# A transformer block on one core: sources turned by 64-row products, maxima by products with the identity in column groups

## The chip, the cores and the metric

The kernel runs on one core of a Trainium2 chip. The metric is the device time of one execution in microseconds. TensorE (PE in the profile; its weight loads are PEld) does the matrix products, VectorE (DVE), ScalarE (ACT) and GpSimd (POOL) the rest, and SyncE (SP) issues nearly all transfers.

## The reference

Sixteen batches of 256 tokens of width 256 pass through one block: self-attention with 16 heads of 16, cross-attention to a context of 256 tokens, and an MLP of width 1024. Layer norms are modulated by a projection of the condition.

```python
def _ln(x):
    mu = jnp.mean(x, axis=-1, keepdims=True)
    var = jnp.var(x, axis=-1, keepdims=True)
    return (x - mu) * jax.lax.rsqrt(var + LN_EPS)
...
c_proj = jax.nn.silu(c) @ W_mod + b_mod
shift_a, scale_a, gate_a, shift_m, scale_m, gate_m = jnp.split(c_proj, 6, axis=-1)
x_norm = modulate(_ln(x), shift_a, scale_a)
qkv = x_norm @ W_qkv + b_qkv
...
attn_w = jax.nn.softmax(jnp.einsum('bhqd,bhkd->bhqk', q, k) * scale, axis=-1)
attn_out = jnp.einsum('bhqk,bhkd->bhqd', attn_w, v)
...
x = x + gate_a[:, None] * attn_out
q_c = _ln(x) @ W_qc + b_qc
kv_c = _ln(context) @ W_kvc + b_kvc
...
x = x + c_attn_out
x_norm2 = modulate(_ln(x), shift_m, scale_m)
h = jax.nn.gelu(x_norm2 @ W_mlp1 + b_mlp1)
x = x + gate_m[:, None] * (h @ W_mlp2 + b_mlp2)
```

## The kernel before

A unit is one attention of one batch: kind "s" for self, "c" for cross. There are 32 units in the list `seq` (line 791): five "s", then "s" and "c" in turn, and five "c" at the end. The MLP of all batches comes after them, with some of its loads and first products among the last units.

The main loop (line 1268) goes over the units n and, within each, over eight beats k (`beat`, line 1103). `keep_in_program_order` holds each engine to the order in which the code issues. A beat handles several units at once:

- **S** (`s_tile`, line 697): scores of unit n + 1 with queries on the partitions, four products of 63 rows, two in each half of the array's rows, into the two banks of the tile `s`. One instruction of DVE then takes the row maxima out of both banks into `u.mx` (tile mx). The next S writes the same two banks.
- **T** (`t_part`, line 741): the transposed scores of unit n, four products of 64 rows into the two banks of the tile `st`. The 64th row carries the negative maximum, so that the exponential on ScalarE (`exp`, line 752) needs no other shift. The next T writes the same banks. The function `visit` (line 1079) issues S, then what it is given as `between`, then T.
- **o** (`av_part`, line 771): in beats 0, 2, 4 and 6, sixteen value products of 128 rows in four column groups of 32.
- **The lanes** (`lane`, `lanes`, `run`, lines 451 to 480): in beats 1, 3, 5 and 7, the projections to q, k, v and the output projection of neighbouring units. Each is cut into two halves of 64 rows; the first half of one operation (upper rows of the array) and the second half of another (lower rows) are issued in turn, twelve products of each, 24 in all.
- **The turning of a source** (`transposed`, line 377): the normalized input of a unit, 256 tokens by 256 features, is transposed by four 128-row products with the identity into one bank (tile psT). Each unit turns one source for unit n + 3 (`q3.T[0]`), half of it in beat 0 and half in beat 2, once the source is marked ready; a unit whose n + 3 is a "c" (`lx`) turns a second one, `lx.T[1]`, whole, in beat 4. ScalarE reads the result in beat 3, or 6.
- **The maxima** (`m_turn`, `m_row`, `m_part`, lines 725 to 739): in beat 0 and beat 4 a half of the maxima, 128 x 16, is transposed by one product (into the second half of the source's bank, a bank psm of its own, or `st`). ScalarE negates it into `m`, and one transfer by SP writes it to the 64th rows of the queries, where T reads it four beats later.

In beat 0 the order on TensorE is S, T, o, maxima, half a turning; in beat 2 S, T, o, half a turning; in beat 4 S, T, o, second source, maxima; in beat 6 S, T, o and one pair of lane products. Ahead of S in beats 0 and 4 ScalarE is given the upper parts of K and Q (`high`, tiles h_k, h_q and the like), so they stand in its queue ahead of the beat's exponential.

Of the kernel before, what the change touches and what calls it, by code (L numbers as in the profile page):

```python
# [10 lines left out]
F32 = mybir.dt.float32  # L11
# [5 lines left out]
P = 128  # L17
# [4 lines left out]
def pixart_block(  # L22
# [53 lines left out]
    DVE.memset(wz, 0.0)  # L76
    ident = const.tile([P, P], F32, name="ident")
    make_identity(nc, ident)
    mhalf = const.tile([P, 2], F32, name="mhalf")
# [297 lines left out]
    def transposed(src, name, scale=None, pool=False):  # L377

        o = Box()

        def place():
            o.ps = ps_gen(f"psT_{name}", SHORT)

        def turn(fs=range(KC)):
            if len(fs) == KC:
                place()
            for f in fs:
                for t in range(NT):
                    PE.transpose(o.ps[:, f * N + t * P:f * N + (t + 1) * P],
                                 src()[:, t, f * P:(f + 1) * P], ident)  # L390

        def high():
            hi = work.tile([P, KC, N], F32R, tag="xTh", name=f"xTh_{name}", bufs=4)
            lo = work.tile([P, KC, N], F32R, tag="xTl", name=f"xTl_{name}", bufs=4)
            o.xT = (hi, lo)
            if scale is None:
                ACT.copy(hi.rearrange("p k n -> p (k n)"), o.ps)
            else:
                for f in range(KC):
                    ACT.activation(hi[:, f], o.ps[:, f * N:(f + 1) * N], AF.Identity, scale=scale[f])  # L400

        def low():
            hi, lo = o.xT
            if scale is None:
# [66 lines left out]
    def lanes(x, y):  # L471


        if x:
            x.ps, x.fresh = ps_gen(f"ps_{x.name}", LONG if x.tok else SHORT), True
        return zip_longest(*(lane(o, half) for half, o in enumerate((x, y)) if o))

    def run(steps, n=12):
        for _ in islice(steps, n):
# [2 lines left out]
    def to_stack(W, src, bias, dst, which, name):  # L482
# [24 lines left out]
        def low():  # L507
            if name == "k0":
                gap(work, 64, "gap_l")
            o.lo = work.tile([P, KC, N], F32R, tag="qkl", name=f"l_{name}", bufs=3)  # L510
            if name == "k0":
                gap(work, 192, "gap_mx")
# [184 lines left out]
    def s_tile(u, g, par, t, bank=None, home=sp):  # L697
# [30 lines left out]
    def m_turn(u, hf, pst=None):  # L728

        if pst is None:  # L730
            pst = ps_gen(f"psm_{u.n}_{hf}", SHORT)
        PE.transpose(pst[:16, :P], u.mx[:, hf].rearrange("p r a t -> p (r a t)"), ident)
        return pst

    def m_row(u, hf, pst):

# [31 lines left out]
            for f in pieces:  # L768
                next(f)

    def av_part(u, g):
# [8 lines left out]
        if g == 3:  # L780
            o_out(u, 1)

    def o_out(u, half):
# [292 lines left out]
    def unit(n):  # L1076
        return units[n] if 0 <= n < nu else None

    def visit(n, k, home=sp, between=None):


        v, e = unit(n + 1), k
# [11 lines left out]
        later.append(lambda: exp(units[n], k))  # L1094

    def spare(n, gate=True):
        p1, _, p3 = (v and v.post for v in map(unit, (n - 1, n - 2, n - 3)))
# [5 lines left out]
    def beat(n, k):  # L1103
# [20 lines left out]
        if k == 6:  # L1124
            if q2 and not n:
                q2.V.keep()
            if p2 and not alone:
                p2.end()
        kp = None
        if k == 5 and lx and n:  # L1130
            kp = lanes(q3.K, None if alone else p2)
        visit(n, k, between=kp and (lambda: run(kp, 2)))
        if k == 0:
            exps()
            if prev:
                av_part(prev, 3)
            if q3 and q3.ready:
                q3.T[0].place()
                pst = m_turn(cur, 1, q3.T[0].ps[:, N:])
                q3.T[0].turn((0,))  # L1140
            else:
                pst = m_turn(cur, 1)
            if prev:
                p1.pull_sums(1)
            m_row(cur, 1, pst)
            if q2:
                q2.K.low()
                q2.K.send_low()
# [3 lines left out]
                p2.low()  # L1152
        elif k == 1:
            exps()
            run(lanes(q2 and q2.Q, q2 and n and q2.V))
            if prev:
                p1.pull_values(1)
            if lc:
# [6 lines left out]
        elif k == 2:  # L1165
            exps()
            if cur:
                av_part(cur, 0)
            if q3:
                q3.T[0].turn((1,) if q3.ready else (0, 1))  # L1170
            if ls:
                ls.ln[0].steps[0]()
            elif prev:
# [24 lines left out]
        elif k == 4:  # L1198
            exps()
            if alone:  # L1200
                p2.end()
            if cur:
                av_part(cur, 1)
            if lx:
                lx.T[1].turn()
            if nxt:
                m_part(nxt, 0, st[:, 0] if lx else None)
            if q2:
                q2.Q.low()
                q2.Q.send_low()  # L1210
# [7 lines left out]
                ls.ready = True  # L1218
        elif k == 5:
            exps()  # L1220
            run(kp or lanes(q3 and q3.K, (None if alone else p2) if n else q2.V))
            if cur:
                o_out(cur, 0)
            if lc:
# [8 lines left out]
        elif k == 6:  # L1233
# [139 lines left out]
```

## Time and profile before

| what | value |
|---|---|
| median of 3 runs | 719.25 us (718.14 to 719.31) |
| span of the profiled execution (no other time of it is given) | 719.7 us |
| TensorE, share of the span | 99% |
| VectorE, ScalarE, GpSimd | 79%, 77%, 72% |
| granted TensorE clock | 0.999 |

How to read it: all instructions are recorded at one helper's line, L51, so groups are told apart by their tiles, written as out<-in. A timeline row gives the start in us from the beginning of the span, the length, the engine, the operation and how many were merged. "<-" in brackets names what ended the engine's idle time before the row. The ends of TensorE's products are modelled, so its times are best taken from one start to the next.

### The profile page before, as it was taken

The numbers are of one execution on the slowest core, as the hardware profiler recorded it, in microseconds if no ns is written. First come the engines' busy times: TensorE is split into PE (matmuls) and PEld (weight loads), VectorE is DVE, ScalarE is ACT, GpSimd is POOL, SyncE is SP. The second block draws the span as 40 slices with busy tenths as digits, with TensorE's granted clock in tenths as the row PEclk, the third lists the DMA queues.
The fourth block names the chain that finished last, engine by engine and source line by source line (L and its number), as shares of the span: only waits on it lengthen the run. The fifth ranks groups of instructions, "written<-read, shape, count | busy, mean of one in ns | idle before, by whom it ended". The sixth has DMA issues, their size and how long they took to land.

```text
span 719.7 us, 22488 instructions
## 1 busy us (share of the span) xinstructions
PE 710.4 (99%) x8993; PEld 592.3 (82%) x8993; DVE 567.8 (79%) x895; ACT 551.7 (77%) x955; POOL 520.6 (72%) x518
## 2 busy tenths in 40 slices
PE   9999999999999999999999999999999999999997
PEld 8777777777877778777787777777779999999997
DVE  5878888888888798888888888888675777777653
ACT  5677888888888788887888888887867677666661
POOL 7655778787776867776686798977857988656651
PEclk9999999999999999999999999999999999999999
DMA  7574455554545456454655656456323132313212
GB/s 236 183 233 157 160 170 178 175 179 160 167 151 196 162 176 191 163 166 153 195 167 176 210 174 195 156 192 196 95 78 103 59 87 61 88 46 88 66 39 74
DMA packets 81548, 106.15 MB, mean 147 GB/s; under 512 B 16610, under 2 KB 44548, under 8 KB 81444
## 3 DMA queue, kind: packets, MB, share of 16 engines
q1 hardware_dynamic: 80548, 104.37, 45.5%
q8 instruction: 71, 1.16, 0.7%
q10 hardware_dynamic: 896, 0.35, 0.2%
q14 instruction: 33, 0.27, 0.1%
HBM read 35.89 MB, written 8.98 MB: 62 GB/s over the span
## 4 chain that ended last, share of the span: by engine, by line
PE 94%; DVE 3%; POOL 2%; issue 0%; ACT 0%; POOLq 0%; ACTq 0%
PE s L51 18%; PE o L51 16%; PE st L51 16%; PE ph L51 12%; PE ps_qc L51 4%; PE ps_kc L51 4%; PE ps_k L51 4%; PE ps_q L51 3%; PE ps_v_c L51 3%; PE ps_v_s L51 3%; PE ps_P_s L51 2%; DVE mx L51 2%; PE ps_P_c L51 2%; PE psT_c L51 2%; PE psT_s L51 2%; PE psT_q L51 1%
## 5 line engine op out<-in xcount | busy, mean ns | idle before, releaser
L51 DVE TENSOR_REDUCE mx<-s 128x4 f32<-128x1024 f32 x252 | 307.9, 1222 | 73.5 <-PE s L51 70.1
L51 ACT ACTIVATE pt<-st 128x1024 f32<-128x1024 f32 x256 | 263.4, 1029 | 51.8 <-PE st L51 51.0
L51 PE MATMUL o<-pt,v 128*32 128x256 f32 x2048 | 137.1, 385 | 0.0
L51 PE MATMUL s<-big 63*128 63x256 f32 x1008 | 116.8, 305 | 1.7 <-DVE st_q L51 0.8
L51 PE MATMUL st<-big 64*128 64x256 f32 (+1 forms) x1040 | 107.7, 282 | 0.8 <-issue 0.4
L51 PE MATMUL ph<-xTh_m,wself 128*128 128x256 f32 x512 | 100.2, 281 | 0.0
L51 POOL TENSOR_TENSOR hl<-hf,hh 128x512 fp32r<-128x512 f32 x60 | 80.1, 1350 | 20.8 <-ACT hh L51 20.8
L51 PEld LDWEIGHTS s<-big 63*128 63x128 f32 x1008 | 77.3, 185 | 21.0 <-issue 7.1
L51 PEld LDWEIGHTS o<-pt,v 128*32 128x32 f32 x2048 | 53.4, 109 | 39.5 <-ACT oT L51 1.3
L51 PEld LDWEIGHTS st<-big 64*128 64x128 f32 (+1 forms) x1040 | 81.2, 186 | 3.6 <-ACT pt L51 1.5
L51 PEld LDWEIGHTS ph<-xTh_m,wself 128*128 128x128 f32 x512 | 82.3, 188 | 1.2 <-issue 0.4
L51 PE MATMUL ph<-xTl_m,wself 128*128 128x256 f32 x256 | 71.1, 278 | 0.0
L51 ACT ACTIVATE hf<-ph,bT 128x256 f32<-128x256 f32 x112 | 47.0, 473 | 22.1 <-PE ph L51 21.9
L51 ACT ACTIVATE hh<-ph,bT 128x256 fp32r<-128x256 f32 x112 | 47.0, 472 | 19.8 <-PE st L51 8.4
L51 PEld LDWEIGHTS ph<-xTl_m,wself 128*128 128x128 f32 x256 | 48.2, 188 | 0.0
L51 PE MATMUL s<-big,hh 128*128 128x256 f32 x256 | 45.6, 278 | 0.0
L51 DVE TENSOR_SCALAR xn_m<-x,mv_m,rs_m 128x256 f32<-128x256 f32 x28 | 33.5, 1237 | 14.8 <-POOL rs_m L51 14.8
L51 POOL TENSOR_SCALAR xn_q<-x,mv_q,rs_q 128x256 f32<-128x256 f32 x32 | 38.9, 1225 | 1.7
L51 POOL TENSOR_SCALAR xn_c<-c,mv_c,rs_c 128x256 f32<-128x256 f32 x32 | 38.9, 1226 | 1.7
L51 PE MATMUL st<-big,hh 128*128 128x256 f32 x224 | 40.0, 278 | 0.0
L51 PEld LDWEIGHTS s<-big,hh 128*128 128x128 f32 x256 | 38.8, 188 | 0.0
L51 POOL TENSOR_SCALAR rs_c<-mv_c 128x2 f32<-128x2 f32 x16 | 3.6, 228 | 48.3 <-DVE mv_c L51 48.2
(230 smaller groups left out, 2133.1 us busy)
## 6 DMA issues: line engine op xcount, KB each, us to landing
big<-h_k SPq DMA_DIRECT2D x32, 256.0 KB
big<-h_kc SPq DMA_DIRECT2D x32, 256.0 KB
big<-h_qc SPq DMA_DIRECT2D x32, 256.0 KB
big<-h_q SPq DMA_DIRECT2D x30, 256.0 KB
big<-l_k SPq DMA_DIRECT2D x16, 256.0 KB
g<-gd SPq DMA_DIRECT2D x16, 256.0 KB
U_s<-oT SPq DMA_DIRECT2D x32, 128.0 KB
R_s<-rd_s SPq DMA_DIRECT2D x16, 256.0 KB
```

The lines of the kernel that those rows point to most:

```text
L51: i = f(*a, **k)
```

## The change

Four things are changed.

1. **Turning.** A source that is ready is turned in two halves of 64 rows each (`half`). For each half, `turning` issues six products: four 64-row transposes of 64 columns and two lane products in the other half of the rows. The first half stands in beat 1 between S and T, beside the second lane's first two products; the second half in beat 2, beside the first lane's last two. For the second source of a unit with `lx` it is beats 5 and 6. The lanes of beats 1 and 5 then run ten steps in place of twelve.
2. **Order of S and T.** In beats 2 and 6, where a second half is turned, T comes first, then the turning, then S (`first_t`).
3. **Maxima.** The row maxima lie in one constant tile `mxs` with 32 columns for a half, 16 of them zero. Two real products with the identity, each in its own group of 32 columns (`m_cols`), replace the transpose. They are issued behind T and ahead of o. The result goes to the bank of the source that is turned next, where there is one. ScalarE negates 64 x 64 values and SP writes them in two transfers (`m_send`), ahead of the copy of o in beat 0.
4. **Fill.** In beat 6 of a unit with `lx` no pair of lane products is issued behind o; all twelve pairs stand in beat 7.

```diff
+        def half(h):
+            rows = slice(64 * h, 64 * h + 64)
+            for f in range(KC):
+                for t in range(NT):
+                    c = f * N + t * P + 64 * h
+                    PE.transpose(o.ps[:, c:c + 64], src()[rows, t, f * P:(f + 1) * P], ident[rows, rows])
+                    yield
...
+    def turning(T, h, beside):
+        t = T.half(h)
+        for f in (t, beside, t, t, beside, t):
+            next(f)
...
-            u.mx = work.tile([P, 2, 2, 4, NT], F32, tag="mx", name=f"mx_{u.n}", bufs=3)
+            u.mx = mxs[u.n % 3][:, :, :16].rearrange("p f (r a t) -> p f r a t", r=2, t=NT)
...
+    def m_cols(u, hf, pst=None):
+        if pst is None:
+            pst = ps_gen(f"psm_{u.n}_{hf}", SHORT)
+        w = mxs[u.n % 3][:, hf]
+        for j in range(2):
+            PE.matmul(pst[32 * j:32 * j + 32, :64], w, ident[:, 64 * j:64 * j + 64], start=True, stop=True,
+                      tile_position=(0, 32 * j))
+        return pst
+
+    def m_send(u, hf, pst):
+        m = work.tile([64, 64], F32R, tag="m2", name=f"m2_{u.n}_{hf}", bufs=1)
+        ACT.mul(m, pst[:64, :64], -1.0)
+        for j in range(2):
+            SP.dma_start(u.q[63:P:64, 4 * hf:4 * hf + 4].rearrange("r a (t q) -> r a t q", t=NT)[..., 64 * j:64 * j + 64].bitcast(F32),
+                         m[32 * j:32 * j + 16].bitcast(F32))
...
+        if first_t:
+            s, t = t, s
         in_turn(*s)
         if between:
             between()
         in_turn(*t)
...
-        kp = None
-        if k == 5 and lx and n:
-            kp = lanes(q3.K, None if alone else p2)
-        visit(n, k, between=kp and (lambda: run(kp, 2)))
+        between = None
+        if k in (1, 5):
+            x, y, T = ((q2 and q2.Q, q2 and n and q2.V, q3 and q3.ready and q3.T[0]) if k == 1 else
+                       (q3 and q3.K, (None if alone else p2) if n else q2.V, lx and lx.T[1]))
...
+            a, b = pair_of(x, y)
+            steps = weave(a, b)
+            if T:
+                held.append((T, a))
+                between = lambda: turning(T, 0, b)
+        elif held:
+            between = lambda: turning(held[0][0], 1, held.pop()[1])
+        visit(n, k, between=between, first_t=k in (2, 6) and between)
+        def rest_of():
+            run(steps, 10 if held else 12)
         if k == 0:
             exps()
+            T = q3 and q3.ready and q3.T[0]
+            if T:
+                T.place()
+            pst = m_cols(cur, 1, T.ps if T else None)
             if prev:
-                av_part(prev, 3)
-            if q3 and q3.ready:
-                q3.T[0].place()
-                pst = m_turn(cur, 1, q3.T[0].ps[:, N:])
-                q3.T[0].turn((0,))
-            else:
-                pst = m_turn(cur, 1)
+                av_part(prev, 3, False)
+            m_send(cur, 1, pst)
             if prev:
+                o_out(prev, 1)
                 p1.pull_sums(1)
-            m_row(cur, 1, pst)
...
+            if lx:
+                lx.T[1].place()
+            if nxt:
+                pst = m_cols(nxt, 0, lx.T[1].ps if lx else None)
             if cur:
                 av_part(cur, 1)
-            if lx:
-                lx.T[1].turn()
             if nxt:
-                m_part(nxt, 0, st[:, 0] if lx else None)
+                m_send(nxt, 0, pst)
...
                 q3.vk = lanes(q3.V, q3.K)
-                run(q3.vk, 1)
+                run(q3.vk, 0 if lx else 1)
```

More of the change, by code (lines that the diff above doesn't have):

```diff
@@ L78, in pixart_block @@
     make_identity(nc, ident)
+    mxs = const.tile([P, 3, 2, 32], F32, name="mxs")
+    POOL.memset(mxs, 0.0)
+    mxs = [mxs[:, i] for i in range(3)]
     mhalf = const.tile([P, 2], F32, name="mhalf")
@@ L390, in turn @@
                                  src()[:, t, f * P:(f + 1) * P], ident)
+        def half(h):
[5 more added lines that the diff above has]
+                    yield
+        o.half = half
         def high():
@@ L475, in lanes, with pair_of, weave @@
             x.ps, x.fresh = ps_gen(f"ps_{x.name}", LONG if x.tok else SHORT), True
-        return zip_longest(*(lane(o, half) for half, o in enumerate((x, y)) if o))
+        return weave(*pair_of(x, y))
+    def pair_of(x, y):
+        return [lane(o, half) if o else iter(()) for half, o in enumerate((x, y))]
+    def weave(*gens):
+        return zip_longest(*gens)
+    def turning(T, h, beside):
+        t = T.half(h)
+        for f in (t, beside, t, t, beside, t):
+            next(f)
     def run(steps, n=12):
@@ L511, in low @@
             if name == "k0":
-                gap(work, 192, "gap_mx")
+                gap(work, 576, "gap_mx")
             for f in range(KC):
@@ L769, in in_turn, with av_part @@
                 next(f)
-    def av_part(u, g):
+    def av_part(u, g, out=True):
         if g % 2 == 0:
@@ L779, in av_part @@
                           start=(c == 0), stop=(c == NT - 1), tile_position=(0, h * 32))
-        if g == 3:
+        if g == 3 and out:
             o_out(u, 1)
@@ L1077, in unit, with visit @@
         return units[n] if 0 <= n < nu else None
-    def visit(n, k, home=sp, between=None):
+    def visit(n, k, home=sp, between=None, first_t=False):
         v, e = unit(n + 1), k
@@ L1094, in visit @@
         later.append(lambda: exp(units[n], k))
+    held = []
     def spare(n, gate=True):
@@ L1154, in beat @@
             exps()
-            run(lanes(q2 and q2.Q, q2 and n and q2.V))
+            rest_of()
             if prev:
@@ L1168, in beat @@
                 av_part(cur, 0)
-            if q3:
-                q3.T[0].turn((1,) if q3.ready else (0, 1))
+            if q3 and not q3.ready:
+                q3.T[0].turn()
             if ls:
@@ L1220, in beat @@
             exps()
-            run(kp or lanes(q3 and q3.K, (None if alone else p2) if n else q2.V))
+            rest_of()
             if cur:
```

2 lines of the change are left out of this document (added).

## The prediction

> **What bounds the kernel now.** I read the page first, for the engines and the chain; then TensorE's timeline over two units in the middle; then DVE and ScalarE over the same stretches; then single tiles.
>
> ```profile
> PE 710.4 (99%) x8993; PEld 592.3 (82%) x8993; DVE 567.8 (79%) x895; ACT 551.7 (77%) x955; POOL 520.6 (72%) x518
> PE 94%; DVE 3%; POOL 2%; issue 0%; ACT 0%; POOLq 0%; ACTq 0%
> L51 DVE TENSOR_REDUCE mx<-s 128x4 f32<-128x1024 f32 x252 | 307.9, 1222 | 73.5 <-PE s L51 70.1
> ```
>
> TensorE ends the chain, so its stream is the time. Two loops lie close behind it. There is one pair of banks for S (tile s) and one for T (tile st): the next S waits until DVE's maximum (1222 ns) has read the last one, the next T until ScalarE's exponential has. A beat has one S and one T. The timeline of TensorE gives the beats (start, length, count); the products of the lanes between them are left out:
>
> ```profile
> 252.24 0.48 PE L51 MATMUL s<-big 63*128 63x256 f32 x4
> 252.56 0.40 PE L51 MATMUL st<-big 64*128 64x256 f32 x4
> 252.89 1.07 PE L51 MATMUL o<-pt,v 128*32 128x256 f32 x16
> 253.89 0.28 PE L51 MATMUL psT_s<-ident,mx 128*16 128x128 f32 x1
> ...
> 254.31 0.50 PE L51 MATMUL s<-big 63*128 63x256 f32 x4
> ...
> 257.89 0.44 PE L51 MATMUL psT_s<-ident,xn_s 128*128 128x128 f32 x2
> 258.26 0.50 PE L51 MATMUL s<-big 63*128 63x256 f32 x4
> 258.60 0.41 PE L51 MATMUL st<-big 64*128 64x256 f32 x4
> ...
> 260.21 0.42 PE L51 MATMUL s<-big 63*128 63x256 f32 x4
> ...
> 275.61 0.41 PE L51 MATMUL s<-big 63*128 63x256 f32 x4
> ...
> 277.19 0.66 PE L51 MATMUL psT_q<-ident,xn_q 128*128 128x128 f32 x4
> 277.73 0.28 PE L51 MATMUL st<-ident,mx 128*16 128x128 f32 x1
> 277.94 0.51 PE L51 MATMUL s<-big 63*128 63x256 f32 x4
> 278.52 0.41 PE L51 MATMUL st<-big 64*128 64x256 f32 x4
> ...
> 283.54 0.45 PE L51 MATMUL s<-big 63*128 63x256 f32 x4
> ```
>
> From S to S, beat 0 of a unit takes 2.07 us, beats 1 and 2 together 3.95, beat 3 1.95; with a second source to turn, beat 4 takes 2.33 and beats 5 to 7 together 5.60. An S takes 0.34 behind 128-row work (258.26 to 258.60); T to o is 0.33 (252.56 to 252.89). An S or a T in a stream of 64-row products takes 0.24 (quoted further down, 492.58 to 492.82), so each change of form costs about 0.1. The 16 value products take 1.00 (252.89 to 253.89). Twelve pairs of lane products take 260.21 - 258.60 - 0.24 = 1.37, or 0.115 a pair.
>
> **What goes.** In beat 0 the maxima and half of the turning cost 0.42 (253.89 to 254.31), in beat 2 the other half 0.37 (257.89 to 258.26); in beat 4 the second source with the maxima costs 0.75 (277.19 to 277.94). In beat 6 one pair of lane products behind o moves to beat 7.
>
> **What comes, on TensorE.** (a) Two maxima products in column groups ahead of o. Their form is that of o, so T to the first of them should be the 0.33 of T to o, with no change after. For themselves I bound them by the rows below: 0.06 (a load-bound pitch) to 0.21 (277.73 to 277.94, a whole transpose of maxima and the change behind it). I take 0.08, nearest to the first, since they load 32 columns and move 64 in two groups side by side. (b) A turning: four 64-row transposes in one half of the rows, two lane products in the other. No row shows them. The nearest is two 16-row transposes, 0.27 in all with 208 ns for one:
>
> ```profile
> 5.24 0.27 PE L51 MATMUL st<-ident,c_sb 16*128 16x16 f32 x2
> L51 PE MATMUL st<-ident,c_sb x2: 208/208/208, 5.2 to 5.3; 16*128 16x16 f32 x2
> ```
>
> That is a pitch of 0.06, so four take 0.25 beside two lane products' 2 x 0.115 = 0.23: I take 0.25, with 0.23 as the lower end and, if the transposes go at the lanes' pitch, 4 x 0.115 = 0.46 as the upper. The four lane products taken (two of each lane) shorten the lanes by two pairs, 0.23, so a source costs 2 x 0.25 - 0.23 = 0.27. The Trainium skill speaks against this: in "TensorE: Matmul & The Clock Gate", section "LDWEIGHTS (loading the stationary operand)", a load's time goes with its columns and not its rows, columns divided by 1.2 in ns, so eight half-height loads of 128 columns cost twice four full ones; by it a turning would be an estimated 4 x 0.107 = 0.43. The 0.06 above, for 128 columns too, does not agree.
>
> **What comes, as waits.** TensorE keeps program order, so whatever waits at its head holds up all behind it. These rows give the loops and ScalarE's queue:
>
> ```profile
> 492.58 0.43 PE L51 MATMUL s<-big 63*128 63x256 f32 x4
> 492.82 0.43 PE L51 MATMUL st<-big 64*128 64x256 f32 x4
> 493.05 1.22 DVE L51 TENSOR_REDUCE mx<-s 128x4 f32<-128x1024 f32 x1 [0.30 <-PE s L51]
> 493.18 1.07 PE L51 MATMUL o<-pt,v 128*32 128x256 f32 x16
> 494.33 0.50 PE L51 MATMUL s<-big 63*128 63x256 f32 x4
> 276.65 1.02 ACT L51 ACTIVATE pt<-st 128x1024 f32<-128x1024 f32 x1
> 278.05 0.27 ACT L51 ACTIVATE m<-st 16x128 fp32r<-16x128 f32 x1 [0.37 <-PE st L51]
> 278.96 1.03 ACT L51 ACTIVATE pt<-st 128x1024 f32<-128x1024 f32 x1 [0.65 <-PE st L51]
> 279.88 0.58 ACT L51 COPY oT<-o 128x512 f32<-128x512 f32 x1
> 284.50 1.02 ACT L51 ACTIVATE pt<-st 128x1024 f32<-128x1024 f32 x1
> ```
>
> At 492.58 stands a beat of S, T, o and nothing else: o, with its 1.00, would let S in at 494.18, but S starts at 494.33, right behind the maximum that ended at 494.27. So S to S is 1.75 at least, with DVE idle before. For T the loop is 0.44 to the exponential (278.52 to 278.96), 1.03 for it, and some 0.05 to TensorE as behind the maximum: 1.52.
>
> - First wait: beats 2 and 6 now run T, turning, S, o. From that S to the next there is only 0.24 + 0.10 + 1.00 = 1.34 of TensorE's work, where S, turning, T, o would have had 1.83. The loop needs 1.75: 0.41 of idle time.
> - Second wait: T in front comes 0.24 + 10 x 0.115 = 1.39 after the T before it, and the loop needs 1.52: 0.13 idle.
> - Third wait: the maxima stand in the bank that the turning writes, so its first transpose (beat 1 or 5) waits for ScalarE's copy of them, which stands behind the exponential. In beat 0 the exponential starts 0.96 behind S (283.54 to 284.50), in beat 4 1.04 (275.61 to 276.65). The next instruction starts 0.92 later (278.96 to 279.88) and the copy takes 0.27; with 0.05 that is 2.20 and 2.28 behind S. TensorE is there at 1.75 + 0.34 = 2.09. Idle 0.11 and 0.19. Behind that transpose stand T, and so the next exponential.
>
> The rows of maxima go out in two transfers in place of one, ahead of the sums in SP's queue. They are read four beats later, over 7 us; a transfer's issue takes this long:
>
> ```profile
> L51 SPq DMA_DIRECT2D big<-m x64: 557/577/630, 28.9 to 523.7; - x64
> L51 PE MATMUL psT_c<-ident,mx x16: 276/277/278, 80.8 to 474.1; 128*16 128x128 f32 x16
> L51 PE MATMUL psT_s<-ident,mx x12: 276/277/278, 49.7 to 379.5; 128*16 128x128 f32 x12
> L51 PE MATMUL st<-ident,mx x16: 272/277/278, 89.3 to 482.5; 128*16 128x128 f32 x16
> ```
>
> 0.58 more on SP twice a unit delays the sums and the low parts behind them, which are used beats later: nothing. Were that cover gone it would be 0.58 a time.
>
> **The sum.** The counts are in the same rows: 16 + 12 = 28 units turn a source in beats 0 to 2, and 16 a second in beats 4 to 6.
> First source: beat 0 is 0.24 + 0.33 + 0.08 + 1.00 = 1.65, held to 1.75 by the loop: -0.32. Beat 1: 0.34 + 0.11 + 0.25 + 0.24 + 1.15 = 2.09. Beat 2: 0.13 + 0.24 + 0.25 + 1.75 = 2.37. Both, against 3.95: +0.51. Beat 3 the same. Together +0.19, times 28: +5.3.
> Second source: beat 4 1.75: -0.58. Beat 5, as beat 1 with 0.19, 2.17; beat 6, as beat 2, 2.37; beat 7, with the pair that beat 6 gives up, 0.34 + 0.24 + 1.38 = 1.96. The three, against 5.60: +0.90. Together +0.32, times 16: +5.1.
> Fifteen units turn only maxima in beat 4, which gains at most their 0.21 less 0.08, but the loop of S holds the beat to 1.75: about -0.04 each, -0.6.
> Sum +9.8. The profiled execution's span, 719.7, is the only time of it shown, 0.45 above the median of 719.25; 719.25 + 9.8 = 729. What is saved on TensorE without any wait, (0.42 + 0.37 - 0.08 - 0.27) x 28 + (0.75 - 0.08 - 0.27) x 16 = 19 us, is more than paid back in waits.
>
> **The rivals.**
> - ScalarE is in time (faster). If the copy of the maxima and the exponentials are never late, the second and third wait go: (0.13 + 0.11) x 28 + (0.13 + 0.19) x 16 = 11.8 less, 717; with 0.02 less in the loop of S (the maximum's 1222 ns and its start 0.47 behind S make 1.69 before TensorE hears of it), 2 x 44 x 0.02 less again, 715. It decides where these waits fall under about 0.05 a source. For it: the exponential at 278.96 found ScalarE idle for 0.65. Against it: the exponentials of beats 0 and 4 do start about 1 us behind S. Chance 0.15.
> - The transposes go at the lanes' pitch, 0.46 a turning: 88 turnings x 0.21 = +18.5, 747. For it: every product in a lane loads 128 columns and none is under 0.115. Against: the 0.06. Chance 0.15. (By the Trainium skill's 0.43 it would be 88 x 0.18 = 16 more, 745.)
> - A transpose and a lane product never run side by side, and each of six changes in a turning costs 0.1: +53, 782. Chance 0.04.
> - The turning doesn't come to pass, since no source is ready in time: about 719. But 28 units already turn half a source in beat 0. Chance 0.02.
>
> **How the numbers follow.** The forecast, 729, has the remaining 0.64, from 721 to 738 by its own unknowns (turning 0.23 to 0.32, third wait 0 to 0.2). The range 715 to 747 takes in the first two rivals. A measurement of this kernel tells about 0.2%, 1.4 us, from no change. Faster by more: the first rival, 0.15, and 0.01 of the forecast. Same: 0.05. Slower: 0.79.
>
> **What would show it.** Right: S in beats 3 and 7 starts just behind the maximum's end, about 1.75 behind the S before it, with TensorE idle 0.4 us; beats 0 to 3 take 8.1 to 8.2 us against 7.97; a turning takes 0.25. The page should have mx as a larger releaser, and DVE a larger share of the chain. Wrong: S to S of 1.4 from beat 2 to 3, or transposes 0.115 apart, or the copy of the maxima early by 0.2.

## The result, and the profile after

| kernel | median, us | runs, us | ratio |
|---|---|---|---|
| before | 718.69 | 717.67 to 719.31 | |
| changed | 740.91 | 739.56 to 741.60 | 1.0306 [1.0287, 1.0324] |

The change makes the kernel 22.2 us slower. The forecast was 729, so the direction held and the loss was more than twice as large; 740.91 also lies above the 721 to 738 that the forecast gave to its own unknowns. The profiled execution of the changed kernel took 740.43 us, 1.8 more than its span of 738.6. The spans of the two traces differ by only 18.9. If as much lies around the span of before, that execution took an estimated 721.5, which is above all runs of before listed here, so the traces understate the loss.

First the page of the changed kernel: the engines, the chain, and the group of the maxima.

```profile
PE 713.6 (97%) x9358; PEld 600.9 (81%) x9358; DVE 564.1 (76%) x895; ACT 543.2 (74%) x955; POOL 521.0 (71%) x519
PE 85%; DVE 11%; DMA 2%; issue 1%; ACT 0%; POOL 0%; ACTq 0%
L51 DVE TENSOR_REDUCE mxs<-s 128x4 f32<-128x1024 f32 x252 | 307.5, 1220 | 98.8 <-PE s L51 97.5
```

TensorE's busy time, with its modelled ends, has not become less (713.6 against 710.4), and DVE's share of the chain has gone from 3% to 11%, as the prediction said it would. DVE itself is no slower: 1220 ns a maximum. Its idle time ahead of the maxima has grown from 73.5 to 98.8. So DVE has no more work than before, and TensorE hardly more; each waits more for the other. The view of the waits shows it (engine and tile that waited, for whom, us in total, times, longest), before and then after:

```profile
PEld s L51 <- DVE mx L51: 5.4, 14, 0.6
PEld st L51 <- ACT pt L51: 1.5, 3, 0.7
```

```profile
PEld s L51 <- DVE mxs L51: 67.7, 114, 0.8
PE s L51 <- DVE mxs L51: 14.2, 45, 0.3
PEld st L51 <- ACT pt L51: 5.5, 27, 0.7
```

A row of PEld is idle time of the weight loads, during which products may still run. The row of PE is time in which, by the modelled ends, no product ran: 45 times 0.32 in the mean, and before has no such row. In the trace 44 of the 45 are the S of beat 3 (28 units) and of beat 7 (16), one behind each second turning. Where the waits stand is seen in the timeline of TensorE over beats 0 to 3 of one unit of the changed kernel (start, length, count; most lane products left out):

```profile
277.72 0.49 PE L51 MATMUL s<-big 63*128 63x256 f32 x4
278.05 0.40 PE L51 MATMUL st<-big 64*128 64x256 f32 x4
278.38 0.25 PE L51 MATMUL psT_c<-ident,mxs 128*32 128x64 f32 x2
278.40 0.41 PE L51 MATMUL o<-pt,v 128*32 128x256 f32 x2
278.45 0.23 PE L51 MATMUL psT_c<-ident,mxs 128*32 128x64 f32 x2
278.51 1.03 PE L51 MATMUL o<-pt,v 128*32 128x256 f32 x14
279.53 0.50 PE L51 MATMUL s<-big 63*128 63x256 f32 x4
279.93 0.24 PE L51 MATMUL psT_c<-ident,xn_c 64*128 64x64 f32 x1
...
280.01 0.35 PE L51 MATMUL psT_c<-ident,xn_c 64*128 64x64 f32 x3
280.17 0.49 PE L51 MATMUL st<-big 64*128 64x256 f32 x4
280.49 0.28 PE L51 MATMUL ps_q<-xTh_s,wself 64*128 64x256 f32 x1
...
281.78 0.50 PE L51 MATMUL st<-big 64*128 64x256 f32 x4
282.12 0.28 PE L51 MATMUL ps_q<-xTl_s,wself 64*128 64x256 f32 x1
...
282.34 0.48 PE L51 MATMUL s<-big 63*128 63x256 f32 x4
282.75 1.07 PE L51 MATMUL o<-pt,v 128*32 128x256 f32 x16
284.13 0.50 PE L51 MATMUL s<-big 63*128 63x256 f32 x4 [0.32 <-DVE mxs L51]
```

The second turning itself is short: 282.12 to 282.34. But from the S behind it to the next there is only o, 1.00 long (282.75 to 283.75), and then TensorE stands until 284.13 for the maximum: S to S is 1.79. In ScalarE's and DVE's timelines over the same stretch stand the releasers of all three waits:

```profile
279.57 0.21 ACT L51 ACTIVATE m<-psT_c 64x64 fp32r<-64x64 f32 x1
...
280.70 1.03 ACT L51 ACTIVATE pt<-st 128x1024 f32<-128x1024 f32 x1 [0.45 <-PE st L51]
```

```profile
282.85 1.23 DVE L51 TENSOR_REDUCE mxs<-s 128x4 f32<-128x1024 f32 x1 [1.31 <-PE s L51]
```

The copy of the maxima ends at 279.78 and the first transpose follows at 279.93. The exponential ends at 281.73 and T follows at 281.78. The maximum ends at 284.08 and S follows at 284.13.

The lengths of the beats, from the starts of S in the timelines of TensorE (means over 11 units with a second source and 11 without, units 2 to 23):

| kernel, units | 0 | 1 | 2 | 3 | 4 | 5 | 6 | 7 |
|---|---|---|---|---|---|---|---|---|
| before, second source | 2.08 | 2.00 | 1.97 | 1.96 | 2.31 | 1.97 | 1.83 | 1.79 |
| changed, second source | 1.82 | 2.77 | 1.79 | 1.96 | 1.75 | 2.93 | 1.80 | 1.96 |
| before, none | 2.10 | 2.00 | 1.95 | 1.96 | 1.79 | 1.96 | 1.84 | 1.89 |
| changed, none | 1.75 | 2.89 | 1.79 | 1.95 | 1.85 | 1.96 | 1.81 | 2.05 |

Beats 0 to 3 lose 0.33 and 0.37 us, beats 4 to 7 lose 0.54 with a second source and 0.19 without. The last S of the last unit but one starts at 539.80 in place of 518.55.

### The profile page after: what moved, and what is told of

It reads as the page before. It is cut to its first block, busy times and chain, and to the rows that moved or that the text cites. A ratio compares the mean times of both kernels' runs of the same rounds, so it can differ in the third digit from the quotient of the medians.

```text
span 738.6 us, 23441 instructions
## 1 busy us (share of the span) xinstructions
PE 713.6 (97%) x9358; PEld 600.9 (81%) x9358; DVE 564.1 (76%) x895; ACT 543.2 (74%) x955; POOL 521.0 (71%) x519
## 3 DMA queue, kind: packets, MB, share of 16 engines
q8 instruction: 74, 1.21, 0.7%
## 4 chain that ended last, share of the span: by engine, by line
PE 85%; DVE 11%; DMA 2%; issue 1%; ACT 0%; POOL 0%; ACTq 0%
PE s L51 19%; PE st L51 16%; PE ph L51 12%; DVE mxs L51 10%; PE o L51 9%; PE ps_q L51 3%; PE ps_kc L51 3%; PE ps_v_c L51 3%; PE ps_k L51 3%; PE ps_qc L51 3%; PE ps_v_s L51 2%; PE ps_P_s L51 2%; PE ps_P_c L51 2%; PE psT_q L51 1%; PE psT_s L51 1%
## 5 line engine op out<-in xcount | busy, mean ns | idle before, releaser
L51 DVE TENSOR_REDUCE mxs<-s 128x4 f32<-128x1024 f32 x252 | 307.5, 1220 | 98.8 <-PE s L51 97.5
L51 ACT ACTIVATE pt<-st 128x1024 f32<-128x1024 f32 x256 | 263.7, 1030 | 102.3 <-PE st L51 102.0
L51 PE MATMUL o<-pt,v 128*32 128x256 f32 x2048 | 141.4, 384 | 0.0
L51 PEld LDWEIGHTS s<-big 63*128 63x128 f32 x1008 | 80.1, 185 | 72.6 <-DVE mxs L51 67.7
L51 PE MATMUL s<-big 63*128 63x256 f32 x1008 | 120.4, 310 | 17.5 <-DVE mxs L51 14.2
L51 PE MATMUL st<-big 64*128 64x256 f32 (+1 forms) x1040 | 115.8, 293 | 0.6 <-ACT pt L51 0.4
L51 PE MATMUL ph<-xTh_m,wself 128*128 128x256 f32 x512 | 99.5, 280 | 0.0
L51 POOL TENSOR_TENSOR hl<-hf,hh 128x512 fp32r<-128x512 f32 x60 | 80.6, 1359 | 19.3 <-ACT hh L51 19.3
L51 PEld LDWEIGHTS st<-big 64*128 64x128 f32 (+1 forms) x1040 | 81.6, 186 | 10.5 <-ACT pt L51 5.5
L51 PEld LDWEIGHTS o<-pt,v 128*32 128x32 f32 x2048 | 66.7, 109 | 21.9
L51 PEld LDWEIGHTS ph<-xTh_m,wself 128*128 128x128 f32 x512 | 81.9, 188 | 1.2 <-issue 0.4
L51 PE MATMUL ph<-xTl_m,wself 128*128 128x256 f32 x256 | 70.9, 277 | 0.0
L51 ACT ACTIVATE hf<-ph,bT 128x256 f32<-128x256 f32 x112 | 47.0, 473 | 21.0 <-PE ph L51 20.8
L51 ACT ACTIVATE hh<-ph,bT 128x256 fp32r<-128x256 f32 x112 | 47.1, 473 | 19.4 <-PE st L51 9.6
L51 PEld LDWEIGHTS ph<-xTl_m,wself 128*128 128x128 f32 x256 | 48.1, 188 | 0.0
L51 PE MATMUL s<-big,hh 128*128 128x256 f32 x256 | 45.2, 277 | 0.0
L51 DVE TENSOR_SCALAR xn_m<-x,mv_m,rs_m 128x256 f32<-128x256 f32 x28 | 33.5, 1237 | 14.8 <-POOL rs_m L51 14.8
L51 POOL TENSOR_SCALAR rs_c<-mv_c 128x2 f32<-128x2 f32 x16 | 3.7, 228 | 56.6 <-DVE mv_c L51 56.5
L51 POOL TENSOR_SCALAR xn_q<-x,mv_q,rs_q 128x256 f32<-128x256 f32 x32 | 38.9, 1225 | 1.7
L51 POOL TENSOR_SCALAR xn_c<-c,mv_c,rs_c 128x256 f32<-128x256 f32 x32 | 38.9, 1225 | 1.7
L51 PE MATMUL st<-big,hh 128*128 128x256 f32 x224 | 39.5, 276 | 0.0
L51 PEld LDWEIGHTS s<-big,hh 128*128 128x128 f32 x256 | 38.7, 188 | 0.0
```

The source lines that it names most:

```text
L51: i = f(*a, **k)
```

## The experiments

W and P in the expectations are theories of each run by itself. The question over all of them: is the loss the order of S and T with its waits, or the turning by halves and the maxima themselves?

**Maxima in other columns of the bank (own_cols).** Is the third wait tied to the columns that the copy reads?

```diff
-            pst = m_cols(cur, 1, T.ps if T else None)
+            pst = m_cols(cur, 1, T.ps[:, 64:] if T else None)
...
-                pst = m_cols(nxt, 0, lx.T[1].ps if lx else None)
+                pst = m_cols(nxt, 0, lx.T[1].ps[:, 64:] if lx else None)
```

> The changed kernel, with the maxima put in columns 64 to 127 of the source's bank, which only the second half of the turning writes: the first transpose no longer has to wait for ScalarE's copy of them. Theory W (the time went into waits of TensorE, and into the cold start behind each): from S to the first transpose the changed kernel takes 0.47 us in the median against 0.34 without a wait, and behind a wait the lane's second product comes 0.22 after the first in place of 0.115. That is 0.13 + 0.08 a source, times 44: about 9 us less, 732. Theory P (the turning's own products are the cost: small transposes among the lane products hold these up): no change, 741.

Measured 742.9 us, ratio to before 1.032 [1.0298, 1.0343]: no gain, and no difference from the changed kernel that the intervals show. The timelines of ScalarE and TensorE show why.

```profile
289.21 0.22 ACT L51 ACTIVATE m<-psT_q 64x64 fp32r<-64x64 f32 x1
```

```profile
289.57 0.24 PE L51 MATMUL psT_q<-ident,xn_q 64*128 64x64 f32 x1
```

The first transpose still starts 0.14 behind the copy's end (289.43), about as in the changed kernel (0.15), so this program keeps the wait, although the copy reads other columns than the first half writes. The run left the wait in place and says nothing of its price.

**T ahead of S also in the beat behind a turned one (t_first_37).** S then stands behind T and o, and the S loop has 0.4 more in it.

```diff
...
+            turned.append(n * 8 + k)
-        visit(n, k, between=between, first_t=k in (2, 6) and between)
+        visit(n, k, between=between, first_t=k in (2, 6) and between or turned[-1] == n * 8 + k - 1)
```

> The changed kernel, with T ahead of S in beats 3 and 7 too where a turning went before. Theory W: TensorE idles 0.39 us between o of beat 2 (or 6) and the next S, because S to S is held to 1.79; T, whose exponential is long done, fills 0.34 of it. S of beat 4 then is held to 1.79 behind that S. Two beats take 3.58 in place of 1.79 + 1.96 = 3.75: 0.17 x 44 = 7 us less, 734. Theory P: 741.

Measured 732.41 us, ratio 1.0176 [1.0154, 1.0197]: W, 8.5 us less than the changed kernel. In its waits the loads of S stand less than half as long and those of T longer, and of the 14.2 in the row of PE only 0.2 is left; in its timeline T and then S follow o without a gap (278.12 + 1.00 = 279.12).

```profile
PEld s L51 <- DVE mxs L51: 32.8, 70, 0.8
PEld st L51 <- ACT pt L51: 23.5, 71, 0.7
```

```profile
278.12 1.07 PE L51 MATMUL o<-pt,v 128*32 128x256 f32 x16
279.12 0.51 PE L51 MATMUL st<-big 64*128 64x256 f32 x4
279.50 0.51 PE L51 MATMUL s<-big 63*128 63x256 f32 x4
```

The gain is not that of the first wait alone. The third wait has become rarer too: the first transpose stands more than 0.40 behind S in 10 of 44 turnings of this trace, in 33 of 44 of the changed kernel's.

**T first in every beat (t_all_own).** The order is the same in all beats, the first turning stands ahead of T, and the maxima stand in columns 64 to 127, as in own_cols.

```diff
-        if first_t:
-            s, t = t, s
-        in_turn(*s)
-        if between:
+        if between and k in (1, 5):
             between()
         in_turn(*t)
+        if between and k in (2, 6):
+            between()
+        in_turn(*s)
...
```

> The changed kernel with all products kept and only their order changed: T ahead of S in every beat, the first half of the turning ahead of T in beats 1 and 5, the maxima in columns 64 to 127. Theory W: no loop of S or T is shorter than TensorE's own work but one (S of beat 2 to S of beat 3, 0.1 idle). Beats 0 to 3: 2.0 + 1.88 + 1.79 + 1.86 = 7.53 against 8.01 before the change, beats 4 to 7 with a second source 7.53 against 7.90, without one 7.25 against 7.48: 0.48 x 28 + 0.37 x 16 + 0.2 x 12 = 22 us less than before the change, 697. Theory P: the turning still costs what it costs, so it stays above the kernel before, 720 or more.

Measured 733.81 us, ratio 1.0196 [1.0171, 1.022]. Beats 1 to 3 fall to 1.88, 1.80 and 1.95, none above those of before (2.00, 1.97, 1.96; all of units with a second source), and the waits have no row in which the products of S stand for its maximum. But beat 0 rises to 2.50: without S ahead of it, the turning comes to the bank early and waits for ScalarE's copy, which stands behind the upper part of Q and the exponential. In all, turnings stand 13.9 us for that copy, 38 times (7.2, 3.8 and 2.9 in the rows of three tiles).

```profile
283.37 0.84 ACT L51 ACTIVATE h_q<-ps_q,bqkv 128x256 fp32r<-128x256 f32 x2 [0.21 <-PE ps_q L51]
284.10 1.02 ACT L51 ACTIVATE pt<-st 128x1024 f32<-128x1024 f32 x1
285.00 0.21 ACT L51 ACTIVATE m<-psT_q 64x64 fp32r<-64x64 f32 x1
```

```profile
285.36 0.24 PE L51 MATMUL psT_q<-ident,xn_q 64*128 64x64 f32 x1 [0.46 <-ACT m L51]
...
287.32 0.41 PE L51 MATMUL st<-big 64*128 64x256 f32 x4
287.57 0.28 PE L51 MATMUL psT_q<-ident,xn_q 64*128 64x64 f32 x2
```

W expected that the loops so freed would end as a gain; one wait taken away made another one late. The last two rows serve further down: a T that did not wait, 0.25 ahead of the second turning.

**The maxima alone (max_only).** The kernel before, with the column products of beat 0, negated and sent as in the change, and nothing else of it.

```diff
...
+            pst = m_cols(cur, 1, T.ps[:, N:] if T else None)
...
-                av_part(prev, 3)
...
-                pst = m_turn(cur, 1, q3.T[0].ps[:, N:])
...
+                av_part(prev, 3, False)
...
+            m_send(cur, 1, pst)
...
```

> The kernel before, with one part of the change alone: in beat 0 the maxima by two products in column groups ahead of o (into columns of the bank that are written in beat 2), negated and sent as in the change; the turning and the order are those of before, beat 4 too. Theory W: this part gains on TensorE, 0.11 for the transposed maxima less 0.03 to 0.06, in 28 units, and makes no wait: 1.5 to 2.3 us less than before, 716.5 to 717.5. Theory P says nothing of it. If the column products were themselves dear, it would be above 719.

Measured 721.31 us, ratio 1.0018 [1.0002, 1.0033]: no gain, against the expectation. Its beat 0 takes 2.12 in units with a second source and 2.06 without, against 2.08 and 2.10.

**The copy of the maxima by DVE (m_dve).** DVE has the copy done before TensorE comes to the bank.

```diff
-        ACT.mul(m, pst[:64, :64], -1.0)
+        DVE.tensor_scalar(m, pst[:64, :64], -1.0, None, ALU.mult)
```

> The changed kernel, with the maxima negated by DVE in place of ScalarE: DVE gets to them right behind its maximum, some 1.7 us behind S, where ScalarE has them copied 2.2 to 2.3 us behind S, so the bank is free when the turning comes to it (2.1 behind S). Theory W: from S to the first transpose 0.34 in place of 0.47, the lane's second product no longer behind a cold start, so T in beats 1 and 5 takes 0.24 in place of 0.32 and its loop 1.52 in place of 1.61: 0.22 x 44 = 10 us less, 731. Theory P (the transposes themselves put the two halves of the rows out of step): T stays 0.32, only 0.13 x 44 = 6 us less, 735.

Measured 737.48 us, ratio 1.025 [1.0223, 1.0278]: 3.4 less than the changed kernel, below what either expected. The timelines of TensorE and ScalarE show the third wait gone and the next T no earlier for it.

```profile
279.44 0.50 PE L51 MATMUL s<-big 63*128 63x256 f32 x4
279.78 0.22 PE L51 MATMUL psT_c<-ident,xn_c 64*128 64x64 f32 x1
...
280.00 0.48 PE L51 MATMUL st<-big 64*128 64x256 f32 x4
...
280.58 1.02 ACT L51 ACTIVATE pt<-st 128x1024 f32<-128x1024 f32 x1 [0.45 <-PE st L51]
...
281.65 0.50 PE L51 MATMUL st<-big 64*128 64x256 f32 x4
```

S to the turning is the plain 0.34 and the turning 0.22, but T to T is 1.65, longer than the 1.61 of the changed kernel: the exponential starts 0.58 behind T here (280.00 to 280.58), there 0.53. The third wait is a small part of the loss.

**Maxima of beat 4 behind o where they have a bank of their own (psm_late).**

```diff
-            if nxt:
-                pst = m_cols(nxt, 0, lx.T[1].ps if lx else None)
+            if nxt and lx:
+                pst = m_cols(nxt, 0, lx.T[1].ps)
             if cur:
                 av_part(cur, 1)
+            if nxt and not lx:
+                pst = m_cols(nxt, 0)
```

> The changed kernel, with the maxima of beat 4 issued behind o, as before the change, in the units without a second source (11 in the middle part). There they go to a bank of their own that DVE has not yet read out when T is done, and all of o stands behind them. Theory W: beat 4 falls from 1.85 back to 1.79 and the unit's later beats no longer run behind DVE: 0.1 to 0.2 x 11, 1 to 2 us less, 739 to 740. Theory P: no change.

Measured 739.61 us, ratio 1.028 [1.0252, 1.0308]: 1.3 us less than the changed kernel, but the two intervals overlap, so the time alone shows no gain. Beat 4 of units without a second source falls from 1.85 to 1.79, as W said. The wait that it takes away is seen in the changed kernel's DVE and TensorE:

```profile
270.09 0.87 DVE L51 SCALAR_TENSOR_TENSOR xTl_s<-psT_s,sc,xTh_s 128x256 fp32r<-128x256 f32 x2
```

```profile
270.59 0.40 PE L51 MATMUL st<-big 64*128 64x256 f32 x4
271.10 0.25 PE L51 MATMUL psm<-ident,mxs 128*32 128x64 f32 x2
```

T to the maxima takes 0.51 in place of 0.33: the bank comes free only when DVE has read the low part of the first source, at 270.96, and o waits behind.

**S first in every beat, first source by halves in beats 1 and 3 (halves_13).** The kernel before, with the first turning in beat 1 between S and T as in the change, and the second in beat 3, also between S and T; the column products of beat 0, copied by DVE. It turns 27 of the 28 first sources so.

```diff
+        if T and k in (1, 3):
...
+            h, side = (0, b) if k == 1 else (1, a)
+            between = lambda: turning(T, h, side)
...
-            if q3:
+            if q3 and not T:
                 q3.T[0].high()
             exps()
+            if T:
+                T.high()
```

> The kernel before, with the first source of a unit turned by the same 64-row products beside lane products, but in beats 1 and 3, each time between S and T: the order of S and T is that of before, and T of beat 2 and S of beat 3 stand between the halves. Its maxima (beat 0) by column products, negated by DVE. The second source and the maxima of beat 4 are those of before. Theory W (the products are cheap, the waits cost): beats 0 to 3 take 1.79 + 1.97 + 1.79 + 1.95 = 7.50 against 8.01, 0.45 to 0.5 x 27: 12 to 13 us less than before, 706. Theory P (the turning is dear wherever it stands): 719 or more.

Measured 743.87 us, ratio 1.0341 [1.0305, 1.0377]: no faster than the change itself. But beats 0 to 3 take 7.87 in units without a second source, less than the 8.01 of before; the loss is in beat 4, 3.06 against 1.79. ScalarE, DVE and TensorE around it:

```profile
304.01 0.83 ACT L51 ACTIVATE xTh_s<-psT_s,sc 128x256 fp32r<-128x256 f32 x2
```

```profile
304.93 0.88 DVE L51 SCALAR_TENSOR_TENSOR xTl_s<-psT_s,sc,xTh_s 128x256 fp32r<-128x256 f32 x2 [1.21 <-PE st L51]
305.72 1.21 DVE L51 TENSOR_REDUCE mxs<-s 128x4 f32<-128x1024 f32 x1
```

```profile
306.99 0.51 PE L51 MATMUL s<-big 63*128 63x256 f32 x4 [0.77 <-DVE mxs L51]
```

I had put the source's upper part (xTh_s) behind the exponential, so DVE's low part, which needs it, stood waiting at the head of DVE's queue, 1.21 us (the view names T, but the instruction reads xTh_s), ahead of the maximum of beat 4. That this order on DVE is the fault was a theory here; the next run takes it out.

**The same with the second half ahead of S (first_halves).** ScalarE can then read the upper part ahead of the exponential, as before.

```diff
-            between = lambda: turning(T, h, side)
+            if k == 1:
+                between = lambda: turning(T, h, side)
+            else:
+                turning(T, h, side)
+                between = None
...
-            if q3 and not T:
+            if q3:
                 q3.T[0].high()
             exps()
-            if T:
-                T.high()
```

> As halves_13, but the second half of the first source is turned in beat 3 ahead of S in place of behind it, and ScalarE reads the upper part of the source ahead of that beat's exponential, as in the kernel before; DVE's read of the low part then no longer stands, waiting for ScalarE, ahead of the maximum of beat 4. W (halves_13 lost its time only in DVE's order: its beats 0 to 3 took 7.86 us against 7.98 before, and beat 4 lost 0.7 to 1.2): beats 0 to 3 about 7.85, beat 4 as before (2.31 with a second source, 1.79 without); with 28 first sources 4 us less than before, 715 us. P (a source turned by halves costs its waits wherever it stands): not below 719, with beat 4 or the beat of the second half over its length of before by 0.15 or more.

Measured 718.93 us, ratio 0.9989 [0.9973, 1.0005]: 25 us less than halves_13, and no change against before that the interval shows. The place of the second half changed as well, but beat 4 without a second source is 1.09 shorter than in halves_13, near the 1.21 that DVE had waited, so that order was the fault. Beats 0 to 3 take 7.81 without a second source and 7.85 with one, as W said, but beat 4 rises to 1.97 and 2.44, as P said (1.79 and 2.31 before). Most of both lies where beat 3 ends: beats 3 and 4 together take 3.78 and 4.24, before 3.75 and 4.27. Beat 0 is 0.33 and 0.27 shorter, and beats 1 and 2 are 0.28 and 0.27 longer. So the halves gain nothing here. TensorE in beats 1 and 2, most lane products left out:

```profile
253.63 0.48 PE L51 MATMUL st<-big 64*128 64x256 f32 x4
253.97 0.38 PE L51 MATMUL ps_qc<-xTh_q,wqch 64*128 64x256 f32 x1
...
255.23 0.29 PE L51 MATMUL s<-big 63*128 63x256 f32 x1
...
255.37 0.28 PE L51 MATMUL ps_qc<-xTl_q,wqch 64*128 64x256 f32 x1
...
255.49 0.40 PE L51 MATMUL s<-big 63*128 63x256 f32 x2
...
256.06 1.07 PE L51 MATMUL o<-pt,v 128*32 128x256 f32 x16
```

T to the lanes takes 0.34 here (253.63 to 253.97), 0.24 in a stream of 64-row products. The next S starts in one half of the rows (255.23) while the other still runs lane products, and o, which needs all rows, starts 0.83 behind that S; it starts 0.57 behind the S of the other half (255.49), as in step. The two halves differ by two lane products. The turning took two from one lane, and the transposes beside them took as long; the other lane still had its twelve, against ten. In the changed kernel both turnings take from the lanes of the same beat, so ten are left in each (280.49 to 281.53). Here the longer lane sets the time, and the two pairs, 0.23, are not saved.

**The second source by halves as well (both_halves).** First half in beat 5 between S and T, second in beat 7 ahead of S; S first everywhere. The maxima of beat 4 are transposed behind o, as before, into the second source's bank; those of beat 0 are copied by DVE.

```diff
+        if k == 5 and L:
...
+            between = lambda: turning(L, 0, b)
...
+        elif k == 7 and L:
+            turning(L, 1, q3.va)
...
```

> As first_halves, and the second source of a unit is turned by halves too, in beat 5 between S and T beside the second lane and in beat 7 ahead of S beside the first; S stays ahead of T everywhere. W (the price of the change is its order of S and T, not the turning by halves): beat 4 falls from 2.31 to about 1.80, beats 5 to 7 rise by 0.3, so 0.2 less for 16 second sources, 3 us, with the 4 of the first sources 712 us. P: 719 or more, because the first half waits for the copy of the maxima in the same bank (0.2 and more a source) or S in beat 0 comes late behind the low part of the second source.

Measured 719.87 us, ratio 1.0005 [0.999, 1.0021]: no difference from before, 21.0 less than the changed kernel. Beat 4 falls to 1.92 and beats 5 to 7 take 2.27, 2.07 and 1.80. Set against its own units without a second source (1.97, 1.95, 1.82, 1.84), a source by halves costs 8.06 - 7.58 = 0.48. In the kernel before, whole, it costs 2.31 + 1.97 + 1.83 + 1.79 - (1.79 + 1.96 + 1.84 + 1.89) = 0.42. These are means, with a few long beats 7 in them (2.55 here; 2.24 and 2.44 before); by the medians of the sums both are 0.52. W's gain did not come. P's number did, but not for P's reasons: the first transposes stand 0.35 behind S in the median, as without a wait, and beat 0 takes 1.82 and 1.84. In its waits the loads of S stand for 17.8 in place of 67.7, and the row of PE has 0.2 in place of 14.2:

```profile
PEld s L51 <- DVE mxs L51: 17.8, 38, 0.6
PE s L51 <- DVE mxs L51: 0.2, 1, 0.2
```

**Three waits of the change undone at once (three_undone).** The edits of t_first_37, m_dve and psm_late together.

> The changed kernel with three of its waits undone at once: T ahead of S also in beats 3 and 7 behind a turned beat (as t_first_37, 8.5 us less), the maxima copied by DVE (as m_dve, 3.4 less), the maxima of beat 4 behind o where they have a bank of their own (as psm_late, 1.3 less). W (these three are separate waits): the gains add up to 13 us, 728 us, still some 8 over the kernel before, which is the longer loop of T in beat 1 to 2 and 5 to 6 (1.6 us against 1.37 of lane work) and T at 0.34 behind each wait. P (one wait hides another): 731 to 733, no better than t_first_37 alone.

Measured 734.59 us, ratio 1.0197 [1.0171, 1.0223]: nearer to P (731 to 733) than to W (728). The three gains do not add up; it is no better than t_first_37 alone (1.0176), in which most of the third wait had gone already. Beats 1 and 5 are where the time stays, 2.79 and 2.78: T to T is 1.66 there, as in m_dve, and was 1.61 with the third wait.

An order S, turning, T in the second beat (2 or 6) wasn't tried. As argued from the program, and not from a run, nothing in it would make the second half's transposes come after the first half's in the one bank that both write from different rows of the array. With T in front, T's wait for the exponential does that. The Trainium skill has the rule behind this, which the prediction did not weigh: in "TensorEngine Tiling (Array Packing)", section "Restrictions and Gotchas", different row tiles cannot access the same PSUM bank at the same time, and the program has to see to it. No run here shows what happens otherwise. Nor was the changed kernel run with its second halves moved and nothing else, which would price the order alone.

## Why the prediction was right or wrong

The direction and its reason held: the loops of S and T, not TensorE's work, set the beats behind a turning (45 waits of 0.32 where before had none), and both_halves, with the same turning and S first, is back at the time of before. Both_halves differs from the changed kernel in more than the order: DVE copies the maxima (3.4 us in m_dve) and those of beat 4 are as before. By these figures the order and its waits carry most of the loss; their exact share is not measured.

The step that failed is the price of beats 0 to 2 behind a turning, and of beats 4 to 6 likewise. The sum had 1.75 + 2.09 + 2.37 = 6.21 for beats 0 to 2; from 277.72 to 284.13 they take 6.41. Four terms are too small, by 0.06, 0.09, 0.10 and 0.04, and three too large, by 0.05, 0.01 and 0.03. Beats 4 to 7 of units without a second source were put at -0.04 and lost 0.19. By its own steps:

| step | predicted | measured in the changed kernel |
|---|---|---|
| beat 0 | 1.75, held by the loop | 1.75 to 1.82; in the unit shown 1.81 (277.72 to 279.53) |
| turning, first transpose to the next product | 0.25 | 0.24 and 0.22 (279.93 to 280.17, 282.12 to 282.34) |
| two maxima products beside o | 0.08 | 0.13 (278.38 to 278.51) |
| first wait: idle of TensorE behind o | 0.41 | 0.38 (283.75 to 284.13) |
| loop of S | 1.75 | 1.79 (282.34 to 284.13) |
| loop of T, beat 1 to 2 | 1.52 | 1.61 (280.17 to 281.78) |
| second wait: end of the lanes to T | 0.13 | 0.14 (281.53 + 0.11 to 281.78) |
| T to the second turning | 0.24 | 0.34 (281.78 to 282.12) |
| third wait, S to the turning less 0.34 | 0.11 | 0.06 (279.53 to 279.93); 0.13 is the median over the trace |
| first source, beats 0 to 3 | +0.19 | +0.33 and +0.37 (8.34 and 8.38 in place of 8.1 to 8.2) |
| second source, beats 4 to 7 | +0.32 | +0.54 |
| neither, beats 4 to 7 | -0.04 | +0.19 |

- **Beat 0 had S too short.** The sum took 0.24 for it. The kernel before has 0.32 in that place (252.24 to 252.56), the changed one 0.33 (277.72 to 278.05). With T at 0.33, the maxima at 0.13 and o at 1.02 that is 1.81, more than the loop of 1.75.
- **The loop of T was too short**, though the wait at its end is the 0.13 foreseen. I took 0.44 from T to its exponential, as in an even stream. Behind a turning T begins at 280.17 and the exponential at 280.70, 0.53 later: the four products of T take 0.49 there, not 0.40 as at 278.05. That is the 0.09.
- **A product behind a wait takes 0.1 longer.** T in front of the second turning has just waited for the exponential and takes 0.34, the price I had put on a change of form alone. In t_all_own, where T did not wait, it takes 0.25 (287.32 to 287.57). I counted no such price on a wait.
- **The first wait was right**, in place and size, and it is the largest single piece: 14.2 us in the row of PE. T_first_37, which fills it with T, took 8.5 us from the whole. S to the next S came out 0.04 longer, with S to o 0.41 (282.34 to 282.75) where I had 0.34.
- **Units without a second source** lose in beat 4 to a wait on a bank that the prediction did not have (1.85 against 1.79 in psm_late). Moving the maxima ahead of o took away the 1.00 of o that had covered DVE's read. In beat 7 the mean hides three long beats of 2.5 to 2.9 in eleven (two of 2.2 to 2.4 before), where S stands for transfers, two of them this one: "PE s L51 <- DMA big<-l_qc: 1.3, 2, 0.8" in the waits of the changed kernel, and no such row before. I had put the second transfer of the maxima at nothing. It now stands in SP's queue ahead of that low part, but m_dve has both transfers and no such row, so whether it is the cause stays open.
- **The work saved is not shown to be wrong.** The prediction put it at 19 us. That both_halves gains nothing does not refute it: there a source costs two turnings (0.22 and 0.27 in the median; 0.48 in all) and the two pairs of lane products are not saved. In the changed kernel they are, but T waits behind them (281.78), so no run shows this saving as time.

Of the rivals, ScalarE in time was wrong: the copy is late, and taking that wait away gave only 3.4 us (m_dve), where the rival had put 11.8 on the second and third wait. The transposes do not go at the lanes' pitch; they stand 0.06 apart. That 740.91 lies inside the outer range is therefore luck: its upper end, 747, came from this rival alone. By the load rule of the Trainium skill's page "TensorE: Matmul & The Clock Gate", section "LDWEIGHTS (loading the stationary operand)", a turning would be an estimated 0.43; 0.24 and 0.22 do not agree. That each change of form in a turning costs 0.1 was closer than its chance of 0.04 said: not six, but T behind the first turning and T ahead of the second are both at 0.34 or near it (280.17 to 280.49 is 0.32) where I had 0.24.

From the means of the beats, 28 x 0.35 + 16 x 0.54 + 15 x 0.19 = 21.3 us. The starts of the last S show the same: 539.80 - 518.55 = 21.25. Set against the sum's +0.19, +0.32 and -0.04, the units with a first source, with a second and with neither miss 4.5, 3.5 and 3.5 us of these. The share of each missed step was not measured apart beyond the runs above, and the gains of t_first_37, m_dve and psm_late do not add up, as three_undone shows.

## What to carry to other kernels

Changing the order of two steps for one beat shortens one engine's loop and lengthens another's: work out both from start to start, for the beat and the one behind it, before counting what the moved work saves. If an ordering forces such a swap, look for a beat where the work fits without it; here both_halves, with the second half moved on, ahead of S, and other edits beside it, is 21 us shorter than the changed kernel. And ask of every wait removed which reader of the same bank, or which instruction at the head of another queue, is late next: halves_13 and t_all_own each lost by it.

## What the runs showed of the hardware that was not expected

- Four 64-row transposes with 128 columns to load start about 0.06 us apart beside lane products 0.115 apart, and a turning behind S or T that does not wait takes 0.21 or 0.22 in the median of every run (0.27 behind o, in first_halves and both_halves).
- Each maxima product is recorded as two loads and two matmuls, 0.13 us for the two products, and the transposed form it replaced stood 0.11 ahead of the next transpose (253.89 to 254.00 in before). This fits that max_only gains nothing.
- With ten lane products in one half of the rows and twelve in the other, the shorter half goes on to S and T by itself, and the next 128-row product waits for the longer: first S to o took 0.83 in place of 0.57.
- A T ahead of a turning takes 0.34 to the next products when it has just waited (281.78 to 282.12), 0.25 when it has not (t_all_own); a T behind a turning takes 0.34 without a wait (first_halves).
